# The opening of a fused attention and FFN block: identity, row loads and the first Q chunks rearranged

## The chip, the cores and the metric

The kernel runs on one core of one Trainium2 chip. The metric is the device time of one execution in microseconds (us). A core has five engines that run in parallel and meet at semaphores: TensorE (PE in the profile; PEld is its weight load), VectorE (DVE), ScalarE (ACT), GpSimd (POOL) and SyncE (SP). In this kernel SP issues nearly all DMAs. All data are float32.

## The reference

The input x has 2 rows of 512 tokens with 512 features. In the reference, cut to what matters:

```
h = layernorm(x)                               # each token, no weights
q, k, v = h @ Wq + bq, h @ Wk + bk, h @ Wv + bv  # 512 -> 4096 = 32 heads of 128
q, k = rms_norm(q, gq), rms_norm(k, gk)        # over all 4096
a = softmax(q k^T / sqrt(128)) v               # per row and head
x = x + layernorm(a @ Wo + bo)
x = x + layernorm(ffn(layernorm(x)))           # base product and gated rank-16 experts
```

## The kernel before

**Data.** A row of x is four tiles of 128 tokens by 512 features, 256 KB each (`load_x`, L80 to L85). `norms` (L113) takes mean and variance of each token on VectorE (`bn_stats`, `bn_aggr`), the square root of the variance plus `epst` on ScalarE (L130), and the reciprocal and a shift on VectorE. `norm_transposed` (L136) applies them on ScalarE (L141), turns each 128x128 block with TensorE and the matrix `ident` (L143), and copies four blocks of 128 features by 512 tokens, `nT`, out of PSUM, on VectorE (L148) and ScalarE (L150).

**Products.** Q, K and V are computed by a seven-product scheme: the two rows of tokens are the two block columns, two pairs of feature blocks and two pairs of heads the other blocks. `token_sums` (L154) makes t1 to t4 from both rows' nT on VectorE. `weight_sums` (L165) makes s1 to s4 from a 1 MB chunk of weights on GpSimd. `project` (L176) loops over 8 chunks of 4 heads. Products 1 and 2 need the first row alone; product 6 needs t2, 7 needs t3, 4 needs t4, 5 needs t1, and 3 needs the second row. Each product makes two 128x512 results, and each result is two matmuls. Results leave PSUM on ScalarE (u1) or VectorE (u2, u3, heads); `keep_it` stores a head to DRAM (keptq, keptk) and adds its square to `accq` or `acck` with ScalarE and GpSimd.

**Order.** TensorE, VectorE, ScalarE and GpSimd run their instructions in the order in which the program is written (`IN_ORDER`); the DMA issues of SP are placed by the scheduler. In chunk 0 of Q the written order is: LN of the first row, products 1 and 2, LN of the second row, token sums, and then the other five products. Before the first LN stand eight loads of x, the first weights `w_q0`, and the constants: `make_identity` (a memset and a select on GpSimd), `ones`, `epst`, `vec` (biases and gains per head column) and `row` (bo, b_base and the threshold's bias, broadcast to all partitions). Between the first LN and the first chunk, VectorE also computes `nbthr`, `gqk`, `same` (16 copies of 32x32 blocks of `ident`, used late in the kernel) and `steps` (differences of biases, for product 7).

**PSUM.** There are eight banks in two rings of four, `ps` and `aux`. Products alternate between the rings, by `pt` without a tag; the LN transposes of both rows use `aux`.

**After Q.** While the Q chunks run, sums for V's and the output's weights are prepared (`value_sums`, `output_sums`); then come the K chunks, with the scaling of the stored Q, and then attention head by head with V's and the output's products between the heads, and the FFN.

Of the kernel before, what the change touches and what calls it, by code (L numbers as in the profile page):

```python
# [9 lines left out]

F32 = mybir.dt.float32
AF = mybir.ActivationFunctionType
ALU = mybir.AluOpType
# [18 lines left out]
def kernel(ctx: ExitStack, tc: tile.TileContext, x, wq, wk, wv, wo, vecs, rows, wbase, gates, bexp, out):  # L32
# [33 lines left out]
    def tt(name):  # L66
        return tmp.tile([P, 512], F32, tag="tmp", name=name)
# [6 lines left out]
    def pt(name, tag=None):  # L74
        if tag is None:
            tag = ("ps", "aux")[turn_of[0] % 2]
            turn_of[0] += 1
        return psum.tile([P, 512], F32, tag=tag, name=name)

    def load_x(b, name):  # L80
        halves = [xpool.tile([P, 2, D], F32, tag="x", name=f"{name}{b}_{u}") for u in range(NT // 2)]
        xts = [halves[t // 2][:, t % 2, :] for t in range(NT)]
        for t in range(NT):
            nc.sync.dma_start(out=xts[t], in_=x[b, ts(t, P), :])
        return xts  # L85
# [7 lines left out]
    xs = [load_x(b, "x") for b in range(B)]  # L93
    wq0 = load_w(wq[:, ts(0, GH * P)], "w_q0")

    ident = const.tile([P, P], F32, tag="ident", name="ident")
    make_identity(nc, ident)
    ones = const.tile([P, P], F32, tag="ones", name="ones")
    nc.gpsimd.memset(ones, 1.0)
    epst = const.tile([P, 3], F32, tag="epst", name="epst")  # L100
    nc.gpsimd.memset(epst[:, 0:1], LN_EPS)
    nc.gpsimd.memset(epst[:, 1:2], RMS_EPS)
    nc.gpsimd.memset(epst[:, 2:3], P * RMS_EPS)

    vec = const.tile([P, 5, H], F32, tag="vec", name="vec")
    nc.sync.dma_start(out=vec, in_=vecs)
    bq, bk, bv = (vec[:, i, :] for i in range(3))
    row = const.tile([P, 2 * D + 1], F32, tag="row", name="row")
    nc.sync.dma_start(out=row, in_=rows.partition_broadcast(P))
    bo_b, bbase_b, bthr = row[:, 0:D], row[:, D : 2 * D], row[:, 2 * D : 2 * D + 1]  # L110
    nbthr = const.tile([P, 1], F32, tag="nbthr", name="nbthr")

# [23 lines left out]
    def norm_transposed(tiles, name, tag):  # L136

        n = wide(f"n_{name}")
        pss = [pt(f"nt_{name}_{c}", tag) for c in range(NK)]
        for i, rs, shift in norms(tiles, name):  # L140
            nc.scalar.activation(n[:, i, :], tiles[i], AF.Identity, bias=shift, scale=rs)  # L141
            for c in range(NK):
                nc.tensor.transpose(pss[c][:, ts(i, P)], n[:, i, ts(c, P)], ident)  # L143
        outs = []
        for c in range(NK):
            o = npool.tile([P, 512], F32, tag="nT", name=f"nT_{name}_{c}")
            if c % 2 == 0:
                nc.vector.tensor_copy(o, pss[c])  # L148
            else:
                nc.scalar.copy(o, pss[c])  # L150
            outs.append(o)
        return outs

    def token_sums(xTs):  # L154

# [20 lines left out]
    def project(xTs, sums, w_src, bias, step, name, pools, keep, accs, parts, between=lambda: None):  # L176

        G = H // GH
        begun = set()
        for g in range(G):
            a11, a12, a22, s1, s2, s3, s4 = parts
            if g + 1 < G:
                w = load_w(w_src[:, ts(g + 1, GH * P)], f"w_{name}{g + 1}")
                parts = weight_sums(w, f"{name}{g + 1}")

            def product(i, a, x, j):
                ps = pt(f"p{i}_{name}{g}_{j}")
                for c in range(2):
                    nc.tensor.matmul(ps, a[:, c, ts(j, P)], x[c], start=(c == 0), stop=(c == 1))  # L194
                return ps

            def column(v, j):
                return v[:, g * GH + j : g * GH + j + 1]

            def tile_of(what, j):  # L200
                return opool.tile([P, 512], F32, tag="o", name=f"{what}_{name}{g}_{j}")

            def head(b, j):
                pool, tag = pools[j // 2 if len(pools) > 1 else 0]
                return pool.tile([P, 512], F32, tag=tag, name=f"{name}{b}_{g * GH + j}")

            def keep_it(o, b, j):
                h = g * GH + j
                if b not in begun:
                    begun.add(b)  # L210
                    nc.scalar.activation(accs[b], o, AF.Square)
                else:
                    sq = tt(f"sq_{name}{b}_{h}")
                    nc.scalar.activation(sq, o, AF.Square)  # L214
                    nc.gpsimd.tensor_tensor(accs[b], accs[b], sq, ALU.add)  # L215
                nc.sync.dma_start(out=keep[b, h], in_=o)

            two = range(2)
            u1 = [tile_of("u1", j) for j in two]
            for j in two:  # L220
                ps = product(1, a11, xTs[0][0:2], j)
                nc.scalar.activation(u1[j], ps, AF.Identity, bias=column(bias, j), scale=1.0)
            for j in two:
                ps = product(2, a12, xTs[0][2:4], j)
                o = head(0, j)
                nc.vector.tensor_tensor(o, ps, u1[j], ALU.add)
                keep_it(o, 0, j)
            if len(xTs) < B:
                xTs.append(norm_transposed(xs[1], "a1", "aux"))
                sums.extend(token_sums(xTs))  # L230
            t1, t2, t3, t4 = sums
            between()
            u2 = [tile_of("u2", j) for j in two]
            for j in two:
                ps = product(6, s2, t2, j)
                nc.vector.tensor_tensor(u2[j], ps, u1[j], ALU.add)
            between()
            u3 = [tile_of("u3", j) for j in two]
            for j in two:
                ps = product(7, s3, t3, j)  # L240
                nc.vector.scalar_tensor_tensor(u3[j], ps, column(step, j), u2[j], ALU.add, ALU.add)
            between()
            for j in two:
                ps = product(4, a22, t4, j)
                o = head(0, j + 2)
                nc.vector.tensor_tensor(o, ps, u3[j], ALU.add)  # L246
                keep_it(o, 0, j + 2)
            between()
            for j in two:
                ps = product(5, s1, t1, j)  # L250
                o = head(1, j + 2)
                nc.vector.tensor_tensor(o, ps, u3[j], ALU.add)
                nc.vector.tensor_tensor(u2[j], ps, u2[j], ALU.add)
                keep_it(o, 1, j + 2)
            between()
            for j in two:
                ps = product(3, s4, xTs[1][2:4], j)
                o = head(1, j)
                nc.vector.tensor_tensor(o, ps, u2[j], ALU.add)
                keep_it(o, 1, j)  # L260
            yield g

    def attention():
        xTs = [norm_transposed(xs[0], "a0", "aux")]
# [18 lines left out]
        for i in range(2):  # L283
            of, to = (v.rearrange("p (g j) -> p g j", j=GH) for v in (vec[:, i, :], steps[:, i, :]))
            nc.vector.tensor_tensor(to[:, :, 0:2], of[:, :, 2:4], of[:, :, 0:2], ALU.subtract)
# [49 lines left out]
        def scalings():  # L335
# [412 lines left out]

    def ffn(b, xs, w, gate_sb, bexp_sb):

        xT = norm_transposed(xs, f"f{b}", "ps" if b == 0 else "aux")
        yield
        hs = wide(f"hs{b}")[:, :, 0 : E * R + E + 1]
        for t in range(NT):
# [106 lines left out]
```

## Time and profile before

| | us |
|---|---|
| median of 3 runs | 1349.68 |
| lowest and highest run | 1347.05, 1354.99 |
| the profiled execution's own time | 1352.03 |
| its span, first to last instruction | 1350.3 |
| TensorE busy (share of the span) | 1300.9 (96%) |
| VectorE busy | 978.9 (72%) |
| ScalarE busy | 533.6 (40%) |
| GpSimd busy | 473.0 (35%) |

The profile is of one execution. Its page gives each engine's busy time, the span in 40 equal slices of about 34 us with a digit for the tenths that an engine was busy, the DMA queues, the chain of work that ended last, and groups of instructions by line. The trace answers further questions by stretch of time: who waited for whom, the instructions in order of time, and busy time with TensorE's mean granted clock (1.00 is full). In timelines, a row gives start, duration, engine, line, operation, output and inputs, shape and count; in brackets stands how long the engine sat idle before it and what ended that. One 128x512 matmul of float32 shows as two matmul records. DMA issues have no busy time of their own on an engine.

### The profile page before, as it was taken

Reading aid. Unit: us, or ns where it says so; the run is one execution under the profiler, and the core shown is the slowest. Engines: PE = TensorE matmul, PEld = TensorE weight load, DVE = VectorE, ACT = ScalarE, POOL = GpSimd, SP = SyncE. Lnnn points to the kernel's source line nnn. Section 1 sums busy time; section 2 is a strip of 40 time slices with the busy share of each in tenths; the row PEclk is TensorE's granted clock in tenths of the full one; section 3 lists DMA queues with packets and bytes.
Section 4 is the critical chain, followed back from the end, with each engine's and each line's share of the span. In section 5 each row is a group of like instructions: output and inputs, shape, how many; then the busy total and the mean of one; then the engine's idle time right before and its main releaser. Section 6 shows DMA issues by size and latency. Waiting matters only on the chain.

```text
span 1350.3 us, 11826 instructions
## 1 busy us (share of the span) xinstructions
PE 1300.9 (96%) x3532; PEld 652.3 (48%) x3532; DVE 978.9 (72%) x1249; ACT 533.6 (40%) x735; POOL 473.0 (35%) x364
## 2 busy tenths in 40 slices
PE   4899999999999999999999999999999999999976
PEld 2344444444444444455555555555555555544443
DVE  5456564787765468887786786886877898899566
ACT  3223222222213144435445445454454565544333
POOL 3388987666566011111122222322312323211000
PEclk9899999999999999999999999999999999999988
DMA  7399897589898766443356566566556565510101
GB/s 266 134 294 335 298 303 279 180 303 320 320 312 316 242 209 203 156 148 125 113 161 172 145 174 165 148 177 173 163 155 188 133 162 125 133 63 24 38 1 62
DMA packets 146128, 250.45 MB, mean 185 GB/s; under 512 B 11793, under 2 KB 39569, under 8 KB 146065
## 3 DMA queue, kind: packets, MB, share of 16 engines
q1 hardware_dynamic: 135984, 231.35, 51.5%
q0 software_dynamic: 10080, 18.35, 8.2%
q8 instruction: 28, 0.46, 0.1%
q14 instruction: 36, 0.29, 0.1%
HBM read 147.43 MB, written 83.89 MB: 171 GB/s over the span
## 4 chain that ended last, share of the span: by engine, by line
PE 62%; DVE 6%; ACT 1%; issue 1%; ACTq 0%; DVEq 0%
PE pss L474 15%; PE o L530 15%; PE v L417 15%; PE psw L580 10%; PE psy L624 2%; PE f L765 2%; PE p_k L194 2%; DVE quarters L493 1%; DVE s L518 1%; ACT s L521 1%; PE f L815 1%; DVE m L484 1%; PE hg L757 1%; DVE y L614 1%; PE psd L507 1%
## 5 line engine op out<-in xcount | busy, mean ns | idle before, releaser
L487 POOL PARTITION_ALL_REDUCE top<-m x64 | 119.0, 1860 | 615.8 <-DVE m L485 615.8
L475 ACT ACTIVATE s<-pss,rk 128x512 f32<-128x512 f32 x256 | 175.8, 687 | 320.1 <-PE pss L474 298.9
L530 PE MATMUL o<-s,v 128*128 128x512 f32 x512 | 231.4, 594 | 6.0 <-ACT s L521 2.6
L474 PE MATMUL pss<-qh,kh 128*128 128x512 f32 x512 | 230.2, 592 | 0.0
L474 PEld LDWEIGHTS pss<-qh,kh 128*128 128x128 f32 x512 | 97.3, 190 | 122.5 <-issue 121.5
L530 PEld LDWEIGHTS o<-s,v 128*128 128x128 f32 x512 | 96.2, 190 | 112.3 <-issue 96.9
L493 DVE TRANSPOSE_TENSOR_REDUCE quarters<-s 128x64 f32<-128x2048 f32 x64 | 147.3, 2302 | 0.0
L518 DVE TENSOR_TENSOR s<-s,top 128x2048 f32<-128x2048 f32 x64 | 146.0, 2282 | 0.0
L521 ACT ACTIVATE s<-s 128x2048 f32<-128x2048 f32 x64 | 121.8, 1903 | 14.0 <-DVE s L518 12.8
L417 PE MATMUL v<-w_v,t 128*128 128x512 f32 x256 | 116.8, 600 | 0.0
L509 DVE RECIPROCAL inv<-psd 128x16 f32<-128x16 f32 x64 | 16.4, 256 | 127.8 <-PE psd L507 127.8
L215 POOL TENSOR_TENSOR accq<-accq,sq_q 128x512 f32<-128x512 f32 x62 | 79.7, 1285 | 54.4 <-ACT sq_q L214 49.8
L214 ACT ACTIVATE sq_q<-q 128x512 f32<-128x512 f32 x62 | 39.0, 630 | 140.2 <-DVE q L246 78.6
L215 POOL TENSOR_TENSOR acck<-acck,sq_k 128x512 f32<-128x512 f32 x62 | 85.4, 1382 | 21.3 <-ACT sq_k L214 18.1
L214 ACT ACTIVATE sq_k<-k 128x512 f32<-128x512 f32 x62 | 38.7, 630 | 135.6 <-DVE k L246 65.0
L194 PE MATMUL p_q<-t,s_q 128*128 128x512 f32 x192 | 88.3, 610 | 3.6 <-DVE t L160 3.6
L417 PE MATMUL v<-w_v,nT_a 128*128 128x512 f32 x192 | 88.3, 601 | 0.0
L580 PE MATMUL psw<-wr,oh 128*128 128x256 f32 x384 | 88.3, 380 | 0.0
L194 PE MATMUL p_k<-t,s_k 128*128 128x512 f32 x192 | 85.0, 592 | 0.0
L580 PEld LDWEIGHTS psw<-wr,oh 128*128 128x128 f32 x384 | 72.5, 190 | 19.8 <-issue 11.5
L484 DVE TENSOR_TENSOR m<-s 128x1024 f32<-128x1024 f32 x64 | 77.8, 1215 | 4.7 <-ACT s L475 4.7
L417 PEld LDWEIGHTS v<-w_v,t 128*128 128x128 f32 x256 | 46.7, 190 | 49.3 <-issue 49.0
(176 smaller groups left out, 1783.3 us busy)
## 6 DMA issues: line engine op xcount, KB each, us to landing
keptq<-q SPq DMA_DIRECT2D x64, 256.0 KB, 6.1
q<-keptq SPq DMA_DIRECT2D x16, 1024.0 KB, 6.4
w_v<-keptw SPq DMA_DIRECT2D x32, 512.0 KB, 4.0
keptk<-k SPq DMA_DIRECT2D x64, 256.0 KB, 6.4
keptqs<-q SPq DMA_DIRECT2D x64, 256.0 KB, 6.7
qh<-keptqs SPq DMA_DIRECT2D x64, 256.0 KB, 3.0
kh<-keptk SPq DMA_DIRECT2D x64, 256.0 KB, 2.7
keptv<-o_v SPq DMA_DIRECT2D x64, 256.0 KB, 3.7
```

What stands on the lines that cost most here:

```text
L194: nc.tensor.matmul(ps, a[:, c, ts(j, P)], x[c], start=(c == 0), stop=(c == 1))
L215: nc.gpsimd.tensor_tensor(accs[b], accs[b], sq, ALU.add)
L417: nc.tensor.matmul(ps, x[c][:, ts(t, P)], w[:, c, :], start=(c == 0), stop=(c == 1))
L474: nc.tensor.matmul(ps, kk[i][:, ts(k, P)], qs[i], start=True, stop=True)
L475: nc.scalar.activation(s[:, k, :], ps, AF.Copy, scale=rks[b][:, k : k + 1])
L484: nc.vector.tensor_tensor(m, s[:, 0:2, :], s[:, 2:4, :], ALU.max)
L487: nc.gpsimd.partition_all_reduce(ms[i], m[:, 0, :], P, ReduceOp.max)
L493: nc.vector.tensor_reduce(quarters.rearrange("p k j -> p (k j)"), ss[i].rearrange("p k (j r) -> p (k j) r", r=32), AX.X, ALU.add, apply_tr ...
L518: nc.vector.tensor_tensor(s, s, top.unsqueeze(1).to_broadcast([P, NT, 512]), ALU.subtract)
L521: nc.scalar.activation(ss[i], ss[i], AF.Exp)
L530: nc.tensor.matmul(po, vs[b, c][:, k, ts(j, P)], ss[i][:, k, :], start=(k == 0), stop=(k == NT - 1))
L580: nc.tensor.matmul(ps[:, t, :], a, right_of[i, g][:, j, :], start=(j == 0), stop=(j == 1))
```

## The change

The identity matrix is made on VectorE: a scan of ones gives each of 128 partitions the numbers of a count over 32 columns, a transpose in 32x32 blocks gives the same count down the partitions, a compare of the two gives `same` (four 32x32 identities beside one another, which the late part of the kernel uses too), and four copies set the diagonal blocks of `ident`. `ones` also moves to VectorE. `epst` stays on GpSimd and is now its first work. One more square root, `root`, is taken on ScalarE at the start; its result is not used.

The second row of x is issued on ScalarE's DMA queue; the first stays on SP's. The load of `row` is written after chunk 0 of Q, `nbthr` and `gqk` after chunk 2.

`norm_transposed` is split: it does the LN and the transposes, and returns a function that makes the copies out of PSUM. `project` is rewritten so that products 1 and 2 of a chunk can be begun ahead (`open_chunk`); its `leave` writes the exits. In Q the order is now: LN of the first row; products 1 and 2 of chunk 0; LN and transposes of the second row; the exits of chunk 0; the copies of the second row; products 1 and 2 of chunk 1; token sums; the exits of chunk 1; and then the other five products of chunk 0, those of chunk 1, and chunks 2 to 7 as before. What is begun ahead uses the `ps` ring only.

In the instruction order of the built program, TensorE's only difference is that the 8 matmuls of chunk 1's products 1 and 2 stand right after the second row's transposes. On VectorE and ScalarE, the LN of the second row stands ahead of chunk 0's exits. On ScalarE the order at the start is table load, `root`, four loads of the second row. On GpSimd an instruction without operands, which stood before the select of `make_identity`, stands before the first weight sum. On SP the order is first row, `w_q0`, `vec`, weights of chunk 1, `row`, and V's weights.

```
-            nc.sync.dma_start(out=xts[t], in_=x[b, ts(t, P), :])
+            (nc.sync, nc.scalar)[b].dma_start(out=xts[t], in_=x[b, ts(t, P), :])
...
-    ident = const.tile([P, P], F32, tag="ident", name="ident")
-    make_identity(nc, ident)
     ones = const.tile([P, P], F32, tag="ones", name="ones")
-    nc.gpsimd.memset(ones, 1.0)
+    nc.vector.memset(ones, 1.0)
...
+    root = const.tile([P, 1], F32, tag="root", name="root")
+    nc.scalar.activation(root, epst[:, 0:1], AF.Sqrt)
+    count = tt("count")
+    nc.vector.tensor_tensor_scan(count[:, 0:32], ones[:, 0:32], ones[:, 0:32], 0.0, ALU.add, ALU.mult)
+    nc.vector.transpose(count[:, 32:64], count[:, 0:32])
+    same = const.tile([P, 4, 32], F32, tag="same", name="same")
+    nc.vector.tensor_tensor(
+        same,
+        count[:, 0:32].unsqueeze(1).to_broadcast([P, 4, 32]),
+        count[:, 32:64].unsqueeze(1).to_broadcast([P, 4, 32]),
+        ALU.is_equal,
+    )
+    ident = const.tile([P, P], F32, tag="ident", name="ident")
+    nc.vector.memset(ident, 0.0)
+    for i in range(4):
+        nc.vector.tensor_copy(ident[ts(i, 32), ts(i, 32)], same[ts(i, 32), i, :])
...
-    nc.sync.dma_start(out=row, in_=rows.partition_broadcast(P))
...
+        def open_chunk(g, tag=None):
+            a11, a12 = parts[g][0:2]
+            ps1 = [product(g, 1, a11, xTs[0][0:2], j, tag) for j in two]
+            ps2 = [product(g, 2, a12, xTs[0][2:4], j, tag) for j in two]
+            u1 = opened[g] = [tile_of("u1", g, j) for j in two]
+
+            def leave():
+                for j in two:
+                    nc.scalar.activation(u1[j], ps1[j], AF.Identity, bias=column(bias, g, j), scale=1.0)
+                for j in two:
+                    o = head(g, 0, j)
+                    nc.vector.tensor_tensor(o, ps2[j], u1[j], ALU.add)
+                    keep_it(o, g, 0, j)
+
+            return leave
+
+        if len(xTs) < B:
+            load_next(1)
+            leave = open_chunk(0, "ps")
+            second = norm_transposed(xs[1], "a1", "aux")
+            leave()
+            xTs.append(second())
+            leave = open_chunk(1, "ps")
+            sums.extend(token_sums(xTs))
+            leave()
+        t1, t2, t3, t4 = sums
         for g in range(G):
...
-            if len(xTs) < B:
-                xTs.append(norm_transposed(xs[1], "a1", "aux"))
-                sums.extend(token_sums(xTs))
-            t1, t2, t3, t4 = sums
...
-        nc.vector.tensor_scalar(nbthr, bthr, -1.0, None, ALU.mult)
...
-        nc.vector.tensor_tensor(gqk, vec[:, 3, :], vec[:, 4, :], ALU.mult)
-        same = const.tile([P, 4, 32], F32, tag="same", name="same")
-        for i in range(4):
-            rows32 = slice(32 * i, 32 * i + 32)
-            for j in range(4):
-                nc.vector.tensor_copy(same[rows32, j, :], ident[rows32, rows32])
...
+        for i in range(2):
+            of, to = (v.rearrange("p (g j) -> p g j", j=GH) for v in (vec[:, i, :], steps[:, i, :]))
+            nc.vector.tensor_tensor(to[:, :, 0:2], of[:, :, 2:4], of[:, :, 0:2], ALU.subtract)
...
+            if g == 0:
+                nc.sync.dma_start(out=row, in_=rows.partition_broadcast(P))
+            if g == 2:
+                nc.vector.tensor_scalar(nbthr, bthr, -1.0, None, ALU.mult)
+                nc.vector.tensor_tensor(gqk, vec[:, 3, :], vec[:, 4, :], ALU.mult)
```

More of the change, by code (lines that the diff above doesn't have):

```diff
@@ L7 @@
 from concourse.bass_isa import ReduceOp
-from concourse.masks import make_identity
 from concourse._compat import with_exitstack
@@ L143, in norm_transposed, with tiles_of @@
                 nc.tensor.transpose(pss[c][:, ts(i, P)], n[:, i, ts(c, P)], ident)
[L144 to L152, printed above, removed]
+        def tiles_of():
+            outs = []
+            for c in range(NK):
+                o = npool.tile([P, 512], F32, tag="nT", name=f"nT_{name}_{c}")
+                if c % 2 == 0:
+                    nc.vector.tensor_copy(o, pss[c])
+                else:
+                    nc.scalar.copy(o, pss[c])
+                outs.append(o)
+            return outs
+        return tiles_of
     def token_sums(xTs):
@@ L184, in project @@
         begun = set()
-        for g in range(G):
[L186 to L219, printed above, removed]
-            for j in two:
[L221 to L227, printed above, removed]
-            if len(xTs) < B:
-                xTs.append(norm_transposed(xs[1], "a1", "aux"))
-                sums.extend(token_sums(xTs))
-            t1, t2, t3, t4 = sums
[L232 to L235, printed above, removed]
@@ new lines, in project, with load_next, product, column @@
+        parts = {0: parts}
+        opened = {}
+        two = range(2)
+        def load_next(g):
+            if g < G:
+                parts[g] = weight_sums(load_w(w_src[:, ts(g, GH * P)], f"w_{name}{g}"), f"{name}{g}")
+        def product(g, i, a, x, j, tag=None):
+            ps = pt(f"p{i}_{name}{g}_{j}", tag)
+            for c in range(2):
+                nc.tensor.matmul(ps, a[:, c, ts(j, P)], x[c], start=(c == 0), stop=(c == 1))
+            return ps
+        def column(v, g, j):
+            return v[:, g * GH + j : g * GH + j + 1]
@@ new lines, in tile_of, with head, keep_it @@
+        def tile_of(what, g, j):
+            return opool.tile([P, 512], F32, tag="o", name=f"{what}_{name}{g}_{j}")
+        def head(g, b, j):
+            pool, tag = pools[j // 2 if len(pools) > 1 else 0]
+            return pool.tile([P, 512], F32, tag=tag, name=f"{name}{b}_{g * GH + j}")
+        def keep_it(o, g, b, j):
+            h = g * GH + j
+            if b not in begun:
+                begun.add(b)
+                nc.scalar.activation(accs[b], o, AF.Square)
+            else:
+                sq = tt(f"sq_{name}{b}_{h}")
+                nc.scalar.activation(sq, o, AF.Square)
+                nc.gpsimd.tensor_tensor(accs[b], accs[b], sq, ALU.add)
+            nc.sync.dma_start(out=keep[b, h], in_=o)
@@ new lines, in project @@
+        if len(xTs) < B:
[8 more added lines that the diff above has]
+        t1, t2, t3, t4 = sums
+        for g in range(G):
+            if g + 1 not in parts:
+                load_next(g + 1)
+            a11, a12, a22, s1, s2, s3, s4 = parts.pop(g)
+            if g not in opened:
+                parts[g] = (a11, a12)
+                open_chunk(g)()
+                del parts[g]
+            u1 = opened.pop(g)
+            between()
+            u2 = [tile_of("u2", g, j) for j in two]
+            for j in two:
+                ps = product(g, 6, s2, t2, j)
@@ L236, in project @@
                 nc.vector.tensor_tensor(u2[j], ps, u1[j], ALU.add)
             between()
-            u3 = [tile_of("u3", j) for j in two]
+            u3 = [tile_of("u3", g, j) for j in two]
             for j in two:
-                ps = product(7, s3, t3, j)
-                nc.vector.scalar_tensor_tensor(u3[j], ps, column(step, j), u2[j], ALU.add, ALU.add)
+                ps = product(g, 7, s3, t3, j)
+                nc.vector.scalar_tensor_tensor(u3[j], ps, column(step, g, j), u2[j], ALU.add, ALU.add)
@@ L242, in project @@
             between()
             for j in two:
-                ps = product(4, a22, t4, j)
-                o = head(0, j + 2)
+                ps = product(g, 4, a22, t4, j)
+                o = head(g, 0, j + 2)
                 nc.vector.tensor_tensor(o, ps, u3[j], ALU.add)
-                keep_it(o, 0, j + 2)
+                keep_it(o, g, 0, j + 2)
             between()
             for j in two:
-                ps = product(5, s1, t1, j)
-                o = head(1, j + 2)
+                ps = product(g, 5, s1, t1, j)
@@ L252, in project @@
+                o = head(g, 1, j + 2)
                 nc.vector.tensor_tensor(o, ps, u3[j], ALU.add)
                 nc.vector.tensor_tensor(u2[j], ps, u2[j], ALU.add)
-                keep_it(o, 1, j + 2)
+                keep_it(o, g, 1, j + 2)
             between()
             for j in two:
-                ps = product(3, s4, xTs[1][2:4], j)
-                o = head(1, j)
+                ps = product(g, 3, s4, xTs[1][2:4], j)
+                o = head(g, 1, j)
                 nc.vector.tensor_tensor(o, ps, u2[j], ALU.add)
-                keep_it(o, 1, j)
+                keep_it(o, g, 1, j)
@@ L261, in project @@
             yield g
     def attention():
-        xTs = [norm_transposed(xs[0], "a0", "aux")]
-        nc.vector.tensor_scalar(nbthr, bthr, -1.0, None, ALU.mult)
+        xTs = [norm_transposed(xs[0], "a0", "aux")()]
         gqk = const.tile([P, H], F32, tag="gqk", name="gqk")
-        nc.vector.tensor_tensor(gqk, vec[:, 3, :], vec[:, 4, :], ALU.mult)
-        same = const.tile([P, 4, 32], F32, tag="same", name="same")
-        for i in range(4):
-            rows32 = slice(32 * i, 32 * i + 32)
-            for j in range(4):
-                nc.vector.tensor_copy(same[rows32, j, :], ident[rows32, rows32])
@@ L282, in attention @@
         steps = const.tile([P, 2, H], F32, tag="steps", name="steps")
-        for i in range(2):
-            of, to = (v.rearrange("p (g j) -> p g j", j=GH) for v in (vec[:, i, :], steps[:, i, :]))
-            nc.vector.tensor_tensor(to[:, :, 0:2], of[:, :, 2:4], of[:, :, 0:2], ALU.subtract)
         keptw = dram.tile([NG // 2, 4, 2, P, 512], F32, tag="w", name="keptw")
@@ L749, in ffn @@
     def ffn(b, xs, w, gate_sb, bexp_sb):
-        xT = norm_transposed(xs, f"f{b}", "ps" if b == 0 else "aux")
+        xT = norm_transposed(xs, f"f{b}", "ps" if b == 0 else "aux")()
         yield
```

## The prediction

> **What bounds the kernel now.** I read the page first: TensorE (PE) is busy for 96% of the span, and the slices show where it is not, in the first and the last.
>
> ```profile
> span 1350.3 us, 11826 instructions
> PE 1300.9 (96%) x3532; PEld 652.3 (48%) x3532; DVE 978.9 (72%) x1249; ACT 533.6 (40%) x735; POOL 473.0 (35%) x364
> ...
> PE   4899999999999999999999999999999999999976
> ...
> DMA  7399897589898766443356566566556565510101
> ```
>
> Between them TensorE sets the pace, so time saved at the start is kept if the other engines and the DMAs can follow. What matters is then when TensorE falls into its steady step. Busy time by stretch (core 0; start:end, length, then each engine's busy time and instructions, granted clock, DMA share, GB/s) answers that:
>
> ```profile
> 0.00:17.68 17.68, 4.32 (x16) 2.87 (x16) 6.08 (x18) 6.08 (x11) 5.67 (x14) 1.00 0.91 316
> 17.68:26.55 8.87, 8.87 (x16) 3.61 (x16) 7.27 (x22) 2.55 (x5) 5.26 (x5) 1.00 0.40 149
> 26.55:39.04 12.49, 4.79 (x19) 2.95 (x18) 10.04 (x26) 5.81 (x11) 1.26 (x1) 0.83 0.50 167
> 39.04:65.32 26.28, 26.28 (x55) 11.43 (x56) 10.07 (x15) 5.78 (x9) 10.04 (x9) 0.88 0.43 149
> 65.32:226.00 160.68, 160.68 (x376) 71.23 (x375) 96.69 (x120) 41.34 (x65) 140.46 (x108) 1.00 0.88 298
> ```
>
> From 39.04 us to the end of Q TensorE has no gap. Before that there are two: 17.68 us until the first product, and 12.49 us of the second row's LN, with 4.79 busy. In the fourth stretch it is busy but at a clock of 0.88. The list of waits for 0 to 60 us names the releasers, and the timeline of the same stretch says why they were late:
>
> ```profile
> POOL ident masks.py:199 <- issue: 9.8, 1, 9.8
> ACT rs_a L130 <- POOL epst L101: 5.5, 1, 5.5
> POOL s_q L170 <- DMA w_q<-in_wq: 1.6, 1, 1.6
> ```
>
> ```profile
> 3.53 0.69 DVE L127 BATCH_NORM_STATS2 st_a<-x 128x6 f32<-128x512 f32 x1 [3.53 <-DMA x<-in_x]
> ...
> 10.89 0.28 POOL masks.py:199 TENSOR_SCALAR_AFFINE_SELECT ident<-ident 128x128 f32<-128x128 f32 x1 [9.82 <-issue]
> 11.14 0.09 POOL L101 MEMSET epst<- 128x1 f32 x1
> ...
> 11.27 0.48 ACT L130 ACTIVATE rs_a<-mv_a,epst 128x1 f32<-128x1 f32 x2 [5.46 <-POOL epst L101]
> ```
>
> The first x tile is there at 3.53 us, but the square root needs epst, which POOL writes only after make_identity, and that stands 9.82 us in front of its second instruction. The whole first LN starts there. Of TensorE alone, the timeline reads:
>
> ```profile
> 30.27 0.66 PE L143 MATMUL nt_a<-ident,n_a 128*128 128x128 f32 x4 [3.72 <-ACT n_a L141]
> ...
> 36.53 1.10 PE L194 MATMUL p_q<-t,s_q 128*128 128x512 f32 x2 [2.16 <-DVE t L160]
> ...
> 39.04 9.27 PE L194 MATMUL p_q<-t,s_q 128*128 128x512 f32 x14 [1.42 <-DVE t L160]
> ```
>
> A product of one head is two matmuls of 128x512, which show as four records; at full clock they are 0.43 us apart, at half clock 0.86. The last row is 14 records in 9.27 us: mostly half clock.
>
> **The change part by part.** The steps are put end to end to the moment when TensorE begins product 6 of chunk 1, which is 65.32 us before. Both kernels have then done the same TensorE work.
>
> *Identity and epst.* POOL loses the ident and ones memsets and the select; epst comes first on POOL (a memset there is 0.1 us, after 0.72), so it is ready near 1 us instead of 11.2. The wait of about 9.8 us does not vanish: in the changed kernel's instruction order the operand-less instruction that stood ahead of the select now stands ahead of POOL's first weight sum. Its cover: those sums wait for w_q until 12.87 anyway, take 10 us for two chunks (eight of 1.27), and product 6 of chunk 0 needs the first two by 31 us below. They would be late only from a POOL start near 28 us.
> VectorE gets the identity: two memsets, a scan, a 32x32 transpose, a compare, four 32x32 copies. The trace has no scan. The nearest rows are the 16 copies of 32x32 that the kernel drops (4.89 us, 0.31 each) and the 128x16 subtraction (0.17). Four copies are 1.2; the five others at 0.1 to 0.5 are 0.5 to 2.5; I take 0.2 each, 2.2 us in all, from 0.75 to 3.0, before the first tile at 3.53. At the upper end LN starts 0.9 late, which the weights' landing below mostly hides. A gain below nothing is excluded for the ident itself, since it now stands in front of the stats on an in-order engine.
> ScalarE gets one more square root, whose table load (1.28 us) now runs during the loads rather than at 4.52; then four DMA issues, about 0.45 each as on SP (3.72 for eight), from about 2.1 to 4.0. The last of these waits for the first x tile (3.53). The first rs activation can run at about 4.5, so ScalarE costs 0 to 0.5.
>
> *Both rows loaded at once.* Row 1 goes on ScalarE's queue, and w_q, vec, w_q1 move up behind row 0 on SP; row moves behind w_q1 and behind nothing urgent (its reader nbthr is now after chunk 2). SP issues a 256 KB tile every 0.43 us (about 600 GB/s) while 260 to 410 GB/s are moved: the issue does not bound. The Trainium skill, "DMA: Bandwidth & Descriptors", "Issuing engines are not separate DMA queues", speaks against the edit: DMAs of several engines share the same 16 DMA engines and only sequencer time is saved. If a queue of its own brought bandwidth, w_q would have only 2 MB before it and be there near 10 us. By the rule the same 3.1 MB must have moved. The page's GB/s of the first slices (0, 208, 261, 279, 332, 382, 411 in 1.5 us steps) reach 3.1 MB at about 11.4, and landing trails by about 1 us. Before, w_q landed at 12.8. I take the rule: 12.3, bounds 11.3 to 13.5. It also costs row 0 something: its third and fourth tile were there at about 6.6 and 7.4 (when SP's issues that wait for them left) and now share with row 1; I take 8.0 for the fourth.
> From its stats to the first product the fourth tile took 17.68 - 12.93 = 4.75 us before, of which about 1 us was a shift of 1.12 instead of 0.16 beside POOL's sums. 8.0 + 4.75 is 12.75, or 11.8 without that. With weights at 12.3, the first product starts at **12.6** (11.6 to 14.5).
>
> *TensorE from there.*
> Chunk 0, products 1 and 2, 16 records with the same cold start as before: 8.87, to 21.5.
> Row 1's 16 transposes: before, four loads took 0.66 to 0.72, so 0.17 each: 2.7, to 24.2. They need row 1 normalised. VectorE gets to it after the two nT copies (near 12.5) and after steps, which now waits for vec; vec lands with w_q or just behind (13.1 before), say 13. The first stats to the last n_a took 27.27 to 33.05 = 5.8 us, and may take 7.5 beside POOL: 19 to 20.5, ahead of 21.5. ScalarE's u1 exits and VectorE's q exits of chunk 0 stand behind this LN; who waits for them is chunk 1's products, which reuse the four ps banks, from 24.2 on.
> Chunk 1, products 1 and 2: 16 records, 58.45 to 65.32 before, 6.9: to 31.1. w_q1 is issued about 1 us earlier than before (7.4) and landed by 17.1 then: covered. Meanwhile VectorE copies nT (two, 1.3) and makes the token sums, 0.65 each; product 6 needs the sixth: 24.0 + 1.3 + 3.9 = 29.2. This was the 2.16 + 1.42 us wait; the chunk 1 products now hide it with 2 us to spare. If that cover fails, it is what is late next.
> The other five products of chunk 0: 40 records at 0.43 = 17.2: to 48.3.
> Sum: 65.3 - 48.3 = **17.0 us**. By place: 5.1 from the earlier first product, 12.49 - 2.7 - 0.86 = 8.9 from the second gap, 3.1 from the half clock after it (38 records from 39.04 to 58.45 took 19.4 instead of 16.3).
>
> *Clock.* The last term is where a rule weighs. After the 3.72 us gap, records stay 0.86 apart up to 45.15, 6.1 us after 39.04. The Trainium skill, "TensorE: Matmul & The Clock Gate", "Part 1: The HAM clock gate", says half rate after an idle window of about 3.4 us and full rate after about 3.4 us of sustained work. By the rule the lost time is 1.7, by the trace 3.1; since both sit in the time before, I use the trace. For the changed kernel the rule says that no gap is long enough to fall back; only if the light transposes counted as idle would chunk 1 begin cold, at 1.7 (rule) to 3.1 (trace). I take 0.
>
> *After Q's start.* Cost of nothing: SP's order changes by a few places, keptq stores of chunk 1 before the rest of chunk 0; x tiles and the 16 o buffers suffice. DMA runs at 0.88 at 298 GB/s in Q and POOL at 140.46 of 160.68; both are paced by TensorE, each with about a tenth to spare, and w_q for chunk 2 is asked for after product 4 of chunk 0 (41 us), 24 us before it is read. The dropped 16 copies and gqk, nbthr (moved to chunk 2) are off TensorE's path. The rest moves up whole: 226.68 (first K product) becomes about 209.7.
>
> Span 1350.3 - 17.0 = 1333.3. The profiled run took 1352.03, 1.7 more than its span, and is 2.35 above the median of 1349.68; against the median that is **1332.7 us**.
>
> **The rivals.**
> *Loads bound the start.* Row 0 or w_q come late because row 1 shares: first product at 15 to 16. For it: DMA share 0.91 in that stretch. Against: same bytes ahead of w_q. Gain 13.6 to 14.6: about 1335.5.
> *Row 1's LN is late and chunk 1 cold.* vec at 16 or slow VectorE beside POOL, TensorE idle 2 to 3 us at 21.5, then 3 at half clock: gain 11, 1338.7.
> *The DMAs give it back.* Q wants its bytes 17 us sooner, at a share of 0.88, with stretches of K at 0.94 (350 to 400 us). TensorE would show waits for w_q or q; half the gain: 1341. Against: 34 to 50 us was nearly idle in DMA.
> *Slower.* steps stands on VectorE in front of row 1's stats and waits for vec, which stands behind 1 MB of w_q on SP. Each us of vec past about 15 moves row 1, hence token sums and everything, by 1 us; slower than before from vec at about 32, and at 40 it gives 1358. The longest landing in the first 40 us is 9.7, so 14 is more likely.
> *It does not do what it says.* The 9.8 us on POOL moves to somewhere that still holds epst or the first LN: then only the reordering gains, about 12: 1337.7.
>
> **How the numbers follow.** Forecast 0.72, loads 0.11, late row 1 0.07, not as said 0.04, DMAs 0.04, slower 0.02. The forecast's bounds are 1329 to 1336, plus about 3 for the spread of the runs (1347.05 to 1354.99). Reaching to the first two rivals gives 1326.5 to 1339.5. A measurement of this kernel can tell about 0.5% (6.7 us) from none. All but half of the DMA rival and the last case are beyond that: faster 0.94, same 0.04, slower 0.02.
>
> **What would show it.** epst before 1.5 us and the first rs near 4.5; first product at 12 to 13.5; no TensorE gap over 1 us between 12.6 and 48; transposes of row 1 right after chunk 0 at about 21.5; token sums done before chunk 1's products end; product 6 of chunk 1 at about 48; first K product at about 210, and every later stage earlier by the same 17. A first product after 15, a gap before row 1's transposes, half clock after them, or a shift that shrinks through Q and K would each make a step wrong.

## The result and the profile after

| | before | changed |
|---|---|---|
| median | 1352.34 us (4 runs, 1347.05 to 1358.08) | 1333.14 us (4 runs, 1333.01 to 1335.98) |
| profiled execution, its span | 1352.03, 1350.3 us | 1335.98, 1334.0 us |
| ratio to before | | 0.9862, 95% interval 0.9834 to 0.9889 |

One execution of experiment 7 below fell into a slow state (1567.21 us at a clock of 0.832, where the others have 0.985 to 0.995) and is left out of its ratio.

The medians are 19.2 us apart, the two profiled spans 16.3. The page after, to be laid beside the first fence of the prediction (span, engines, and TensorE and DMA in 40 slices):

```profile
span 1334.0 us, 11818 instructions
PE 1296.3 (97%) x3532; PEld 651.2 (49%) x3532; DVE 973.7 (73%) x1242; ACT 533.6 (40%) x736; POOL 472.1 (35%) x361
...
PE   7999999999999999999999999999999999999976
...
DMA  7789978598997765533456565565656555511001
```

TensorE's row differs in its first two digits alone: 7 and 9 instead of 4 and 8. TensorE alone, in the timeline of the first 60 us:

```profile
7.00 1.11 PE L157 MATMUL nt_a<-ident,n_a 128*128 128x128 f32 x4 [7.00 <-ACT n_a L155]
9.48 3.03 PE L157 MATMUL nt_a<-ident,n_a 128*128 128x128 f32 x12 [1.37 <-ACT n_a L155]
12.65 8.42 PE L215 MATMUL p_q<-nT_a,w_q 128*128 128x512 f32 x16
20.91 1.91 PE L157 MATMUL nt_a<-ident,n_a 128*128 128x128 f32 x16
22.66 7.03 PE L215 MATMUL p_q<-nT_a,w_q 128*128 128x512 f32 x16
29.53 7.03 PE L215 MATMUL p_q<-t,s_q 128*128 128x512 f32 x16
...
46.69 7.03 PE L215 MATMUL p_q<-t,s_q 128*128 128x512 f32 x16
```

The rows are the steps of the prediction: chunk 0, row 1's transposes, chunk 1's opening, product 6 of chunk 0, product 6 of chunk 1. None from 12.65 us on has a wait in brackets. What stood in front of the first LN and of the first product, on all engines:

```profile
0.72 0.10 POOL L98 MEMSET epst<- 128x1 f32 x1 [0.29 <-POOLq L895]
...
0.86 1.34 ACTq L83 DMA_DIRECT2D x<-in_x  x3
...
1.85 0.73 DVE L118 COPY ident<-same 32x32 f32<-32x32 f32 x4
...
3.59 0.69 DVE L141 BATCH_NORM_STATS2 st_a<-x 128x6 f32<-128x512 f32 x1 [1.01 <-DMA x<-in_x]
...
4.54 0.29 ACT L144 ACTIVATE rs_a<-mv_a,epst 128x1 f32<-128x1 f32 x1 [2.32 <-DVE mv_a L142]
...
12.24 1.26 POOL L188 TENSOR_TENSOR s_q<-w_q 128x512 f32<-128x512 f32 x1 [11.37 <-DMA w_q<-in_wq]
12.65 0.50 PEld L215 LDWEIGHTS p_q<-nT_a,w_q 128*128 128x128 f32 x2 [0.54 <-DVE nT_a L164]
```

epst and ident are ready before the first tile is read at 3.59, and the first square root of LN runs at 4.54 instead of 11.27. GpSimd's start-up wait now lies in the 11.37 us in front of its first weight sum, which is put down to w_q. w_q had landed at 11.8 (9.2 us after its issue at 2.59). In seven of the ten profiles that have the wait at this place the sum starts 0.08 us behind the landing, here 0.45, so some of the start-up wait may show. It costs nothing: product 6, the first to need these sums, runs at 29.53. The last row says what the first product waited for: for nT, the end of row 0's LN, and not for w_q.

Not all of it is kept. First K product: 226.68 before, 208.06 after, 18.6 us earlier. First V product: 422.68 and 406.50, 16.2 earlier. The 2.4 us are lost at one place, the last K chunk (timeline of TensorE; the first row is of before, the next of after):

```profile
398.57 7.10 PE L194 MATMUL p_k<-nT_a,w_k 128*128 128x512 f32 x16 [1.78 <-DVE q L347]
```

```profile
380.89 8.61 PE L215 MATMUL p_k<-nT_a,w_k 128*128 128x512 f32 x16 [2.72 <-DVE q L380]
```

The wait is 0.94 us longer, and the 16 records behind it take 8.61 us instead of 7.10, at half clock for a while.

### The profile page after: what moved, and what is told of

Its sections match the earlier page's. It is cut to its first block, busy times and chain, and to the rows that moved or that the text cites. A ratio compares the mean times of both kernels' runs of the same rounds, so it can differ in the third digit from the quotient of the medians.

```text
span 1334.0 us, 11818 instructions
## 1 busy us (share of the span) xinstructions
PE 1296.3 (97%) x3532; PEld 651.2 (49%) x3532; DVE 973.7 (73%) x1242; ACT 533.6 (40%) x736; POOL 472.1 (35%) x361
## 4 chain that ended last, share of the span: by engine, by line
PE 64%; DVE 6%; ACT 1%; issue 1%; ACTq 0%; DVEq 0%
PE pss L515 15%; PE o L571 15%; PE v L458 15%; PE psw L621 11%; PE psy L665 2%; PE f L806 2%; PE p_k L215 2%; DVE quarters L534 1%; DVE s L559 1%; ACT s L562 1%; PE f L856 1%; PE hg L798 1%; DVE y L655 1%; PE psd L548 1%; DVE m L525 1%
## 5 line engine op out<-in xcount | busy, mean ns | idle before, releaser
L215 PE MATMUL p_q<-t,s_q 128*128 128x512 f32 x192 | 85.0, 592 | 0.0
```

## The experiments

Each ratio is to the kernel before on the same chip, with its 95% interval. The kernel before ran from 1346.87 to 1359.55 us over these chips, so for differences of a few us the place in the profile is the better evidence.

**1. The identity part alone, on the kernel before.**

```
 (before)
-    make_identity(nc, ident); nc.gpsimd.memset(ones, 1.0); epst behind them
-        same by 16 copies
+    ones, epst, root, count, same, ident as in the change
```

> The kernel before with the identity part alone: count, transpose and compare on VectorE, epst first on GpSimd, the early square root; both rows on SP and the old order in chunk 0. Theory (the start is bound by epst behind make_identity, then by the landing of the first weights): first product at 12.8 us, where w_q lands behind both rows on one queue, against 17.68 before; everything after it as before, so about 4.9 us gained, profiled span about 1345.4. Rival (the start is bound by the row loads sharing with row 1): a first product at 12.7 only because of a late fourth tile, whose stats would then start after 8 us. Rival (the wait on GpSimd only moves): first product not before 15.

Measured: 1346.81 us, ratio 0.9962 (0.9947 to 0.9977), span 1344.9. First product, TensorE timeline:

```profile
12.59 9.13 PE L210 MATMUL p_q<-nT_a,w_q 128*128 128x512 f32 x16 [1.30 <-DMA w_q<-in_wq]
```

Now w_q is what ends the wait, row 0's transposes having ended 1.3 us before. The gaps behind chunk 0 (3.72 us) and at the first token sum (2.16) are as before; at the second it is 0.46 instead of 1.42. The first K product comes at 220.29, 6.4 earlier, 5.1 of them from the first product.

**2. The new order and the second queue, with make_identity.**

```
 (changed)
-    ones, root, count, same, ident on VectorE
+    make_identity ahead of epst on GpSimd; same by 16 copies behind row 0's LN
```

> The changed kernel with make_identity back on GpSimd ahead of epst, and the 16 copies for same back on VectorE (behind the first row's copies): the new order and the second queue alone. Theory (parts add up): first product at 17.7 as before, chunk 0's two products about 8.5 to 26.2, transposes 1.9 to 28.1, chunk 1's two products to 35.0, product 6 of chunk 1 at 52.2 against 65.32 before and 46.69 with everything: about 13 us gained over before, span about 1337 to 1339. Rival (the 16 copies, 5 us on VectorE, delay row 1's LN): row 1's stats start at 24, transposes wait until 29 to 31, gain 8 to 10.

Measured: 1340.82 us, ratio 0.9926 (0.9896 to 0.9956), span 1339.0. First product at 20.17, not 17.7: the wait in front of the select was 11.51 us this time, against 9.82 in the kernel before. From there the order does what it should: transposes at 29.45, chunk 1 at 31.19, product 6 at 38.06, with no gap. First K product at 216.59, 10.1 earlier. Parts 1 and 2 give 6.4 + 10.1 = 16.5 of the 18.6. The 2.1 that are missing are about the size of part 2's slower start, 2.5 us (20.17 against 17.68).

**3. One chunk begun early instead of two.**

```
 (changed)
-            leave = open_chunk(1, "ps")
             sums.extend(token_sums(xTs))
-            leave()
```

> The changed kernel without products 1 and 2 of chunk 1 being begun early: token sums follow the second row's copies directly. Theory (chunk 1's two products are what covers copies and token sums): TensorE ends row 1's transposes at 22.7 and waits for t2 until about 26 and again until 28.5; the gap of 3.3 us is long enough for half clock afterwards, 1.7 to 3.1 more; product 6 of chunk 1 at about 54 instead of 46.69, so 7 to 8 us slower than the changed kernel. Rival (most of the gain came from beginning chunk 0 ahead of row 1's LN, the second chunk is decoration): under 3 us slower.

Measured: 1341.91 us, ratio 0.9926 (0.9899 to 0.9953). TensorE timeline:

```profile
25.57 1.89 PE L215 MATMUL p_q<-t,s_q 128*128 128x512 f32 x2 [2.77 <-DVE t L178]
28.08 8.49 PE L215 MATMUL p_q<-t,s_q 128*128 128x512 f32 x14 [0.62 <-DVE t L178]
```

The token sums are what TensorE waits for, and half clock follows (8.49 us for 14 records; 6.2 at full clock). First K product at 214.94, 6.9 later than with two chunks: the theory had 7 to 8, the rival under 3.

**4. Row 1 behind the first weights.**

```
 (changed)
-            (nc.sync, nc.scalar)[b].dma_start(out=xts[t], in_=x[b, ts(t, P), :])
+            nc.sync.dma_start(out=xts[t], in_=x[b, ts(t, P), :])
-    xs = [load_x(b, "x") for b in range(B)]
+    xs = [load_x(0, "x")]
     wq0 = load_w(wq[:, ts(0, GH * P)], "w_q0")
...
     nc.sync.dma_start(out=vec, in_=vecs)
+    xs.append(load_x(1, "x"))
```

> The changed kernel with row 1 on SP again, but behind the first weights and vec: order row 0, w_q, vec, row 1, weights of chunk 1. Theory (row 1 on a second queue takes bandwidth from row 0 and from the first weights, and is not needed before 13 us): row 0's fourth tile is read by 6.7 us instead of 8.49, w_q lands near 9 instead of 12.2, first product at about 10.3 instead of 12.65; row 1 lands by about 12.5, its LN ends near 19, chunk 0's products end at 18.9: product 6 of chunk 1 at about 45 instead of 46.69, 1.5 to 2.3 us faster. Rival (a second queue has its own worth: row 1 then lands too late): TensorE idle over 2 us before row 1's transposes, no gain or a loss.

Measured: 1330.72 us, ratio 0.9856 (0.9816 to 0.9897), span 1329.6. Row 0's fourth tile was read at 6.57 instead of 8.49, and the first weight sum began at 9.36 instead of 12.24 (w_q itself landed at 8.9 and 11.8):

```profile
9.36 1.26 POOL L189 TENSOR_TENSOR s_q<-w_q 128x512 f32<-128x512 f32 x1 [8.48 <-DMA w_q<-in_wq]
...
10.73 7.49 PE L216 MATMUL p_q<-nT_a,w_q 128*128 128x512 f32 x16
18.05 1.99 PE L158 MATMUL nt_a<-ident,n_a 128*128 128x128 f32 x16
```

First product 1.9 us earlier, as much as the fourth tile, with nT again what it waits for; first K product at 205.46, 2.6 earlier, and row 1 is not late.

**5. Row 1 on SP, at its old place.**

```
 (changed)
-            (nc.sync, nc.scalar)[b].dma_start(out=xts[t], in_=x[b, ts(t, P), :])
+            nc.sync.dma_start(out=xts[t], in_=x[b, ts(t, P), :])
```

> The changed kernel with row 1 back on SP's queue between row 0 and the first weights, all else as changed. Theory (the two queues share one bandwidth, so the second queue buys no landing time and costs row 0 a little): row 0's fourth tile read near 7.3 us instead of 8.49, w_q landing at 12.3 to 12.8 instead of 12.2, first product at 12.3 to 12.9 against 12.65, time within 1 us of the changed kernel. Rival (the second queue is what brought the first product forward): first product at 14 or later, 1.5 to 3 us slower.

Measured: 1336.09 us, ratio 0.987 (0.985 to 0.989). Fourth tile read at 7.46, w_q landed at 12.75, first product at 12.89 (waiting for w_q), first K product at 207.47, span 1334.0 like the changed kernel's. The second queue is worth nothing that can be seen: with it w_q landed 0.95 us earlier and the fourth tile was read 1.03 later, and the first product moved by 0.24.

**6. Only epst moved, on the kernel before.**

```
 (before)
+    epst and its three memsets
     ident = const.tile([P, P], F32, tag="ident", name="ident")
     make_identity(nc, ident)
...
-    epst and its three memsets
```

> The kernel before with only the three epst memsets written ahead of make_identity on GpSimd. Theory (epst, not the identity, held row 0's LN; but the transposes need the identity and that still comes at about 11 us): the normalised tiles are ready near 10, the 16 transposes start at 11 to 11.5 and run through in 2 to 3 us, first product at 14.0 to 14.7 instead of 17.68, so 3 to 3.6 of the 5.1 us come from three memsets alone; time 3 to 4 us under before. Rival (the wait on GpSimd is bound to its first instruction after start, and moves ahead of epst): no change.

Measured: 1353.06 us, ratio 0.9992 (0.9978 to 1.0006): no gain that can be seen. The theory's start was right, its sum was wrong. The first product does come at 13.23. The timelines of VectorE and TensorE in its profiled run say where the time went:

```profile
14.71 8.14 DVE L272 COPY same<-ident 32x32 f32<-32x32 f32 x16
...
24.24 0.68 DVE L127 BATCH_NORM_STATS2 st_a<-x 128x6 f32<-128x512 f32 x1
```

```profile
13.23 7.78 PE L194 MATMUL p_q<-nT_a,w_q 128*128 128x512 f32 x16
27.24 4.09 PE L143 MATMUL nt_a<-ident,n_a 128*128 128x128 f32 x16 [6.22 <-ACT n_a L141]
```

The 16 copies for same, 4.89 us in the kernel before, take 8.14 here, and row 1's stats stand behind them: the gap after chunk 0 grows from 3.72 to 6.22 us. The copies begin 4.4 us earlier than in the kernel before and end only 1.2 earlier, because their end hangs on GpSimd's sums (see the last section). In that run 3.1 us were left at the first K product; over 20 runs nothing was. Part of the 3.1 is chance: the wait in front of the select was 7.92 us in this run and 9.82 in that of the kernel before. What took the rest was not found.

**7. The copies put back into the changed kernel.**

```
 (changed)
         gqk = const.tile([P, H], F32, tag="gqk", name="gqk")
+        for i in range(4):
+            rows32 = slice(32 * i, 32 * i + 32)
+            for j in range(4):
+                nc.vector.tensor_copy(same[rows32, j, :], ident[rows32, rows32])
```

> The changed kernel with the 16 copies of 32x32 into same put back on VectorE, between row 0's nT copies and row 1's LN (they rewrite what is there). Theory (in the kernel before they were off TensorE's path, but in the new order row 1's LN has only chunk 0's products as cover, so VectorE's queue there counts): the copies take 4 to 8 us from 13.1, row 1's stats start at 18 to 21 instead of 13.55, its transposes end at 25.5 to 28.5 instead of 22.66, TensorE idles 2 to 5 us, perhaps at half clock after: first K product 3 to 7 us later than 208.06. Rival (row 1's LN has slack enough): under 1 us later.

Measured: 1339.73, 1340.16 and 1345.14 us, ratio 0.992 (0.9892 to 0.9948), profiled run 1339.73; first K product at 214.68, 6.6 later than changed. VectorE, GpSimd's last weight sum, and TensorE:

```profile
13.25 9.16 DVE L311 COPY same<-ident 32x32 f32<-32x32 f32 x16
...
20.99 1.29 POOL L191 TENSOR_TENSOR s_q<-w_q,s_q 128x512 f32<-128x512 f32 x1
...
25.44 0.82 PE L157 MATMUL nt_a<-ident,n_a 128*128 128x128 f32 x4 [4.15 <-ACT n_a L155]
```

That `same` now falls out of the count is worth about as much as the second chunk. It is so only with the early start: in experiment 2 the same copies stood at the same place and TensorE did not wait, since chunk 0 began at 20.17 there and covered them.

**8. Idle time filled, on the kernel before.**

```
 (before)
+                fill(4, "fill0")     # 128x512 matmuls of ident and nT into one bank, not read
                 xTs.append(norm_transposed(xs[1], "a1", "aux"))
+                fill(2, "fill1")
                 sums.extend(token_sums(xTs))
```

> The kernel before with idle TensorE time filled by matmuls whose result is not read: four of 128x512 between chunk 0's first products and row 1's transposes, two more between those transposes and product 6. No other work moves. Theory (beside the plain gaps, the gaps cost half clock afterwards, and how long it stays is a matter of luck from run to run; that is the last term of the sum and also the spread of the runs before): product 6 of chunk 0 runs its records 0.43 us apart at once, the first K product comes 3 to 4 us before 226.68, the clock of the runs goes from 0.986 to 0.991 up to 0.993 to 0.995, the median falls by 4 to 7 us and the spread of 10 us shrinks to about 4. Rival (the clock is set by the light transposes or by something else in the run): clock and spread as before, time up to 1 us longer.

Measured: 1348.66 us, ratio 0.9969 (0.9956 to 0.9982), and clocks of 0.992 to 0.995 where the kernel before had 0.987 to 0.991. The waits at the token sums, and what follows (TensorE timeline):

```profile
34.53 1.10 PE L194 MATMUL p_q<-t,s_q 128*128 128x512 f32 x2 [0.75 <-DVE t L160]
37.04 6.28 PE L194 MATMUL p_q<-t,s_q 128*128 128x512 f32 x14 [1.41 <-DVE t L160]
```

14 records in 6.28 us, where they took 9.27: the 3 us of half clock are real, and are gone when the idle time is filled. The first K product came at 221.69, 5.0 earlier, of which 1.6 are a first product that happened to come at 16.13. The medians differ by 3.9, just under the 4 to 7 expected. The spread did not shrink (1345.49 to 1351.79, beside 1349.62 to 1355.47), so that part of the theory fell.

**9. Scalings of stored Q spread evenly over K chunks 1 to 7.**

```
 (changed)
         def scale_some():
-            for _ in range(2):
-                if scale_steps:
-                    scale_steps.pop(0)()
+            if scale_steps:
+                scale_calls[0] += 1
+                calls = (NG - 1) * 5
+                due = -(-NG * B * GH * scale_calls[0] // calls)
+                while scale_steps and NG * B * GH - len(scale_steps) < due:
+                    scale_steps.pop(0)()
```

> The changed kernel with the 64 scalings of stored Q spread evenly over the 35 gaps of K chunks 1 to 7 (at most 2 in a gap, 64 in all) instead of 2 in each gap until they run out. Theory (the 2.4 us that are lost between the first K product and V come from a scaling on VectorE that waits for its stored Q at a DMA share of 0.94, holds up the exits behind it and so TensorE, for 2.72 us plus 1.6 us of half clock): the wait on VectorE falls under 0.5 us and TensorE has no gap from 12.65 us to V; span 2.7 to 4.3 us shorter than the profiled 1334.0, or 0 to 3 less than the typical run. Rival (DMA as such is full there): the wait stays or moves to another chunk and the time does not change.

Measured: 1330.95 us, ratio 0.9833 (0.9814 to 0.9853), span 1330.6. TensorE has no wait in K; first V product at 402.21, 4.3 us before the changed kernel's. DMA in K by stretches of 20 us, changed kernel first, then this one:

```profile
340.00:360.00 20.00, 20.00 (x48) 8.76 (x48) 17.64 (x24) 4.13 (x8) 12.72 (x10) 1.00 1.01 356
360.00:380.00 20.00, 18.17 (x43) 7.78 (x41) 13.63 (x20) 5.84 (x10) 9.35 (x7) 1.00 0.95 319
380.00:400.00 20.00, 19.11 (x41) 8.54 (x42) 9.76 (x13) 4.90 (x8) 18.48 (x14) 0.91 0.89 320
```

```profile
340.00:360.00 20.00, 20.00 (x48) 8.91 (x47) 14.93 (x19) 3.72 (x7) 11.75 (x9) 1.00 0.97 338
360.00:380.00 20.00, 20.00 (x48) 8.85 (x47) 17.83 (x23) 3.87 (x8) 12.35 (x10) 1.00 0.83 282
380.00:400.00 20.00, 20.00 (x48) 8.82 (x47) 14.90 (x18) 5.96 (x10) 14.79 (x11) 1.00 0.93 346
```

A DMA share of 1.01 becomes 0.97, and TensorE's 18.17 and 19.11 of 20 become 20.

**10. Both improvements.** The edits of 4 and 9.

> Row 1 late on SP (row 0, first weights, vec, row 1) together with the evenly spread scalings. Theory (the two are independent): first product near 10.7, product 6 of chunk 1 near 44.1, no gap of TensorE in K, first V product near 400 instead of 406.50: span about 1327 to 1328.5, some 22 us under before. Rival (DMA is full in K whatever the spread): as row 1 late alone, span about 1329.6.

Measured: 1330.52 us, ratio 0.9829 (0.9805 to 0.9853), span 1329.1, 0.6 over the top of what was expected: K has no gap, but one of 0.53 for V's weights appears, and product 6 of chunk 1 came at 45.38 and not near 44.1. By the medians the two edits together gain no more than either alone (1330.72, 1330.95 and 1330.52). To compare both edits with the changed kernel, the two ran on one chip in 5 rounds:

> The changed kernel as it is, beside the next one on one chip. Theory: span 1331 to 1335, ratio to before 0.984 to 0.988; the wait of a scaling in K is there again (TensorE idle 1.5 to 3 us before the last K chunk), with or without half clock after it.

> Row 1 late on SP and evenly spread scalings, the same kernel as before under a new name, to compare with the changed kernel on one chip. Theory (the early first product is worth about 1.3 to 1.9 us and the missing wait in K 2 to 4): 3 to 5 us under the changed kernel in the profile, 2 to 4 in the medians. Rival (the gains are lost in V and attention, which start at a DMA share near 0.8): under 1 us.

Measured: changed 1335.67 us (1332.02 to 1341.76), ratio 0.9865 (0.9836 to 0.9894); with both edits 1329.96 (1329.73 to 1332.28), ratio 0.9822 (0.9799 to 0.9846). In the profiled runs TensorE waits 0.8 us in K in the changed kernel, and not at all in the other; the spans are 1330.2 and 1328.2, 2.0 apart and not the 3 to 5 expected; that run of the changed kernel was the shortest of its six. The medians are 5.7 apart, more than expected. The changed kernel's other runs had clocks down to 0.990, those with both edits 0.993 to 0.995. So this version beats both, and is the steadier one. That its steadiness comes from the missing wait in K fits the clocks; the longer runs of the changed kernel were not profiled, so it is not shown.

Not taken out one by one were the later load of `row`, the early square root, and the later `nbthr` and `gqk`.

## Why the prediction was right, step by step

*Start.* epst at 0.72, first square root of LN at 4.54 (said: 4.5), first product at 12.65 (12.6). The identity on VectorE took 1.8 us (2.2). The number of the first product is better than its reason. The prediction took w_q, at 12.3, for what comes last. w_q landed at 11.8, and row 0 came last: its fourth tile was read at 8.49 (8.0), and LN took 4.2 us from there to the first product (4.75, or 3.8 without the long shift). Both were within their bounds. The rule on shared DMA engines held against the hope in a second queue: experiments 5 and 4 show that the queue brings nothing and the order 2.6 us. The forecast called the loads' sharing a small cost to row 0; it did not ask what a better order would give.

*Covers.* GpSimd's start-up wait cost nothing, as said; vec did not hold up VectorE (steps at 13.11); row 1's last normalised tile was done at 20.7, just ahead of the transposes at 20.91. The sixth token sum ended at 28.5, 1.0 us before product 6, not 2. So both covers are near their edge, 5.9 us of sums and copies behind 6.9 of chunk 1, and row 1's LN behind chunk 0; experiments 3 and 7 show what their loss costs. The rivals that needed a late vec or late loads had no part in it.

*One step was incomplete.* The prediction called the dropped 16 copies off TensorE's path. That was so in the kernel before. With an early chunk 0, VectorE's queue between the two LNs is on it, and the copies would have cost 6.6 us (experiment 7). The sum was right only because they had gone.

*Sizes.* Chunk 0 and the transposes took 12.65 to 22.66 = 10.0 us, said 8.87 + 2.7 = 11.6. The transposes were sized at 0.17 each, from rows of four that took 0.66 to 0.72; the 0.72 is from the start, at half clock, and the 0.66 holds the whole length of the last of the four. They ran 0.11 apart right behind dense products. And the cold start was 0.6 shorter. So 18.6 us were gained at the start of K instead of 17.0.

*What was given back.* 2.4 us in the last K chunk. This is the rival of the DMAs in small, in K and not in Q: the wait already in the kernel before, 0.94 longer, and then 1.5 us of half clock, which the clock step took for impossible. On VectorE a scaling of stored Q waits for a landing, and the exits behind it come late (first row before, second after):

```profile
394.02 1.42 DVE L347 SCALAR_TENSOR_TENSOR q<-q,gqk,rq 128x512 f32<-128x512 f32 x2 [1.78 <-DMA q<-keptq]
```

```profile
376.35 1.42 DVE L380 SCALAR_TENSOR_TENSOR q<-q,gqk,rq 128x512 f32<-128x512 f32 x2 [1.38 <-DMA keptk<-k]
```

That the pace of the scalings is the cause, experiments 9 and 10 show: none of the three profiles with the even spread has a TensorE wait in K. Of the eleven without it nine have one, of 0.77 to 4.25 us (that of experiment 8 is put down to K's weights), and those of experiments 2 and 6 have none. Which landing holds the scaling is not settled, since the profile names stored Q in the kernel before and a store of K in the changed one; nor is it shown whether fuller DMAs or a fuller VectorE does it.

So two terms were off, by +1.6 and -2.4, and nearly cancel, which is luck: span 1334.0 against 1333.3. The forecast of the median, 1332.7 against 1333.14, was lucky too. It started from 1349.68, the median of three runs, where four have 1352.34, and took off 17.0 where the medians differ by 19.2. They differ by more than the profiled spans (16.3) mainly because the profiled run of the changed kernel was the longest of its four; the other three have spans of 1331.2 to 1331.4. Whether these lost less in K is not shown, as they were not profiled.

## What to carry to other kernels

When an order is changed so that one engine's work covers another's, read again what else stands in that engine's queue: work that was free before may be what is late next. A small constant (here three memsets of 0.1 us) belongs ahead of the first slow instruction of its engine, though moving it alone brought nothing that could be seen here (experiment 6). Load in the order of first use; a second queue brought no earlier start here.

## What the runs showed of the hardware

*Idle time and the clock.* In the last K chunk TensorE's wait differs from kernel to kernel. Waits of 1.60, 1.78, 1.80 and 1.92 us left the next 16 records at 7.10 to 7.11 us, full clock. Waits of 2.06, 2.72, 3.18 and 4.25 us were followed by 8.80, 8.61, 8.65 and 9.63. So about 2 us of idle time was enough here to lose 1.5 to 2.5 us more. The busy time by stretch shows how the clock went, for the changed kernel and then for the kernel before:

```profile
377.09:380.50 3.41, 1.08 (x3) 0.19 (x1) 3.41 (x7) 0.00 (x0) 0.00 (x0) 1.00 1.05 405
380.51:383.92 3.41, 3.03 (x4) 1.51 (x5) 2.17 (x4) 0.00 (x0) 2.95 (x3) 0.50 0.70 269
383.92:387.33 3.41, 3.41 (x9) 1.47 (x9) 0.00 (x0) 0.00 (x0) 3.41 (x4) 1.00 0.72 175
```

```profile
396.68:400.09 3.41, 1.63 (x5) 0.83 (x5) 3.41 (x6) 0.00 (x0) 1.52 (x1) 1.00 1.05 402
400.09:403.50 3.41, 3.41 (x10) 1.50 (x9) 0.26 (x1) 0.00 (x0) 3.33 (x4) 1.00 0.53 78
```

Within each of the 14 traces the clock changes only at points that lie whole multiples of 3.41 us apart (at 31.45, 34.86, 38.28 and 45.10 in the kernel before). Cut into such stretches, all traces agree: every fall to half clock, 39 in all, follows a stretch in which TensorE was idle for 2.06 us or more, and no stretch with 1.95 or less was followed by a fall. So a wait that lies across such a point counts in two parts: of the 3.72 us behind chunk 0 in the kernel before, 1.5 lay in one stretch, which no fall followed, and 2.2 in the next, which one did. Since the points lie elsewhere in each run, the same wait may cost half clock in one run and not in the next. The prediction had taken the 3.4 us window of the Trainium skill ("TensorE: Matmul & The Clock Gate", "Part 1: The HAM clock gate") as the least gap that matters. Its length agrees with these stretches, but a stretch need not be idle throughout; the measurement decides.

*Copies beside GpSimd.* A 32x32 copy on VectorE took 0.18 us while GpSimd was idle (four in 0.73). Beside GpSimd's 1.27 us weight sums 16 copies took 3.85, 4.89, 6.09, 8.14 and 9.16 us (experiment 2, the kernel before, experiments 8, 6 and 7). The traces show why: of the single copies some last 0.16 to 0.19 us, the others 1.15 to 1.29, and each of these ends within 0.05 us of the end of a GpSimd sum. Once the sums are over, all take 0.16 to 0.18. So wherever the copies began, they ended 0.1 to 1.5 us after GpSimd's last sum (22.3 to 23.0). The Trainium skill, "SBUF — State Buffer", "Who interferes with whom", says that a VectorE copy in its two-port mode and a GpSimd instruction shut each other out for a whole instruction, which fits.

*GpSimd's start.* The wait in front of GpSimd's select was 9.82, 11.51 and 7.92 us in three kernels (before, experiments 2 and 6), and 8.27 in experiment 8, whose program is that of the kernel before up to there. So it differs from run to run. What sets it stays open.
